# A two-layer convolution block on one core: the places of chains, of a projection and of a rank multiply in a planned order, and the buffers of the last stage

## The chip, the cores and the metric

The kernel runs on one core of one Trainium2 chip. The metric is the device time of one execution in microseconds (us); the median of several runs counts. Lower is better.

## The reference: what is computed

The input x has 4 images of 64 channels, 256 x 256 pixels, float32. Two layers follow each other, each with a residual (x = x + layer(norm(x)), where the norm is a group norm over 32 groups of two channels):

```python
# layer 0, on gn(x)
h = gelu(conv3x3(x, c1_w) + c1_b)
xa, k = split(conv1x1(h, c2_w) + c2_b)            # 64 channels each
xs = gelu(depthwise 1x3 then 3x1 taps of xa)
gate = softmax(mean(xs) @ gate_w.T), the two largest of three kept
out = xs + sum over e of gate_e * w3_e((w2_e k + b2_e) * (w1_e xs + b1_e)) + ...   # ranks 2, 4, 8
return proj(out)
# layer 1, on gn(x)
h = relu(batchnorm(conv3x3(x, quantised w1)))
h = batchnorm(conv3x3(h, quantised w2))
return relu(h + x)
```

The gate of an image needs the mean of xs over the whole image, the norm of layer 1 needs all of an image's layer 0, and the two batch norms need all four images. These are the borders in the program.

## The kernel before: how the work is laid out

**Tiles.** An image is held as 128 partitions (64 channels times two row parities) by 128 row pairs by 256 columns. A step of layer 0 takes four row pairs, so an image has NOCT = 32 steps; a chunk is CPAIR = 8 row pairs (1 MiB), and an image has NCH = 16 chunks.

**The plan.** The functions `plan_front`, `plan_stats`, `plan_out` and `plan_conv1` write no instruction. They put calls into a table under a pair (step, order) with `at`, or the pieces of a generator with `at_each`. The table is then walked sorted by step and order (end of the code shown below), and every call emits its instructions on all engines. The order on TensorE (PE), VectorE (DVE), GpSimd (POOL) and the DMA-issuing SyncE (SP) is kept as written; that of ScalarE (ACT) too, from four steps ahead of conv1. So the order number of a call sets at once the place of its matmuls on PE, of its vector work on DVE and of its DMAs on SP. Image b's layer 0 takes the steps from 32b on; conv1 of layer 1 begins at CONV1 = 128 and takes 65 steps per image. Past CONV1 the last steps of image 3's front are stretched (`tail`).

**Layer 0, the front.** A step of row group n does: two thirds of the 3x3 convolution into PSUM bank c (`front_conv_a`, L452 through `rounds` and `quarter`), the rest of it (`front_conv_b`), a butterfly in PSUM on ACT and DVE (`front_butterfly`, L561 to L563), gelu (`front_h`, L569); three steps later the taps into bank a (`front_taps_a`, `front_taps_b`) and their horizontal part on DVE (`front_taps_h`: L619, L622, L625), gelu into xs (`front_xs`, L639); a step or two later the projection of xs (`front_proj`), whose result is added to x on DVE (L673) and stored to t1_d. Every fourth step `front_k` makes the first rank factor from h (matmuls L649, evacuated on ACT, L657) and `front_q` the second from xs (matmuls L687); DVE multiplies the two (L689) and SP stores them to low_d.

**The tick.** `divide` (L443) emits a one-column memset on POOL that waits for PE's latest matmul, and the next `rounds(..., divided=True)` on PE waits for that memset. `front_conv_b` and `front_taps_b` are such rounds. It parts matmuls into different halves of one bank.

**Layer 0, the back.** As soon as the gate of an image is known (`gate`, a generator of three pieces), `out_slot` takes each half chunk, two row pairs by two: the experts' last matmul on the stored ranks (ps_o, L758), added to t1_d's chunk on DVE (L766), statistics (L768), and a store to y_d. For images 0 to 2 this runs beside the next image's front, one `out_slot` per step from the fourth step on, at order 2. `out_end` makes the norm of layer 1 from the statistics (matmuls ps_m_y, L282, and ps_v_y, L291), `stats_end` that of the next image's layer 0.

**Banks.** Of the PSUM there are four tiles of 4 KB per partition: two of tag c, one of tag a, one of tag p (`BANKS`, L76). `front_proj`, `front_k`, `front_q`, `out_slot` and the small matmuls of gate and norms all use the one p.

**Layer 1.** conv1 reads y_d in chunks through a ring (`dense_in`, four buffers shared with layer 0's `chunk_in`), normalises (ACT), splits and sums pixels (`conv1_add`, `conv1_split`, `conv1_sums`, on ACT, DVE and POOL), and convolves with 128x128 matmuls (L310; banks c, and a or p); `leave` (L335, L336) takes the result out, which goes to h1_d. The second convolution does the same from h1_d. Its results stay in SBUF for the last KEEP = 11 chunks (L58) and go to h2_d for the others (store at L1116).

**The end.** After the second batch norm is known, 64 chunks are finished: y is loaded (L1167), ACT and DVE combine it with h2 (L1179 to L1181), the result is stored (L1183). The chunks that stayed come first; as their buffers come free, the others are reloaded from h2_d (L1188). y is loaded AHEAD = 4 chunks ahead at the emission, into the three or so buffers of the ring and two of a pool `end` in turns of five.

Of the kernel before, what the change touches and what calls it, by code (L numbers as in the profile page):

```python
# [57 lines left out]
KEEP = 11  # L58
# [5 lines left out]
def conv_preact_kernel(ctx: ExitStack, tc: tile.TileContext, io, col128, colset, col64):  # L64
# [7 lines left out]
    ring = ctx.enter_context(tc.tile_pool(name="ring", bufs=4))  # L72
# [27 lines left out]
    def chunk_in(name):  # L100

        t = ring.tile([P, RING], F32, tag="in", name=name)
        return t[:, 0 : CPAIR * PW].rearrange("p (a b) -> p a b", b=PW)

    def dense_in(name, n):

        return ring.tile([P, RING], F32, tag="in", name=name)[:, 0 : n * W].rearrange("p (a b) -> p a b", b=W)
# [30 lines left out]


# [42 lines left out]
    av = const.tile([P, 3, C], F32, name="av")  # L182
    sv_sum, sh_sum, sh_bias, tap_bias = (column(n) for n in ("sv_sum", "sh_sum", "sh_bias", "tap_bias"))
    end, ends = column("end", 2), column("ends", 2)
    outer = const.tile([P, 2, W], F32, name="outer")
    wk = const.tile([P, 2, 2, 32], F32, name="wk")
    both = const.tile([P, P], F32, name="both")
    k_bias = column("k_bias")
    pw3 = const.tile([P, C], F32, name="pw3")
    pb3 = column("pb3", 3)  # L190
    wq = {n: const.tile([P, 5, 2 * P], F32R, name=f"{n}_q") for n in ("w1", "w2")}
# [200 lines left out]
    def stats_group(b, g):  # L392
        if g == 0:
            st_x[b] = stat.tile([P, NG, 6], F32, tag="st_x", name=f"st_x{b}", bufs=1)
        t = x_in[b, g // CG]
        i = g % CG * GP
        nc.vector.bn_stats(st_x[b][:, g, :], t[:, i : i + GP, :])  # L397
# [37 lines left out]
    xs_of, hs, xss, k_sb, pooled, open_c, open_a, open_t = {}, {}, {}, {}, {}, {}, {}, {}  # L435
# [27 lines left out]
    def front_alloc(b, k):  # L463
# [3 lines left out]
        else:  # L467
            xs_of[b, k] = chunk_in(f"x_{b}_{k}")
# [190 lines left out]
    def front_proj(b, n):  # L659

        ps = bank("p", f"ps_p_{b}_{n}")
        proj = c128("proj")

        rounds(
            *(
                [((ps[:, i], i ^ s, i, proj, xss[b, n][:, s].rearrange("p (a b) -> p a b", b=W), (0, GP)), dict(start=True, stop=True))]
                for i in range(2)
                for s in range(2)
            )
        )  # L670
# [24 lines left out]
    def gate(b):  # L695
# [10 lines left out]
        nc.vector.tensor_copy(lg, ps[:, 0:9])  # L706
        mx = stat.tile([P, 1], F32, tag="s2", name=f"mx_{b}")
# [42 lines left out]
    def out_slot(b, k, s):  # L750


        if k == s == 0:
            st_y[b] = stat.tile([P, NG, 6], F32, tag="st_y", name=f"st_y{b}")
# [33 lines left out]
    def conv1_load(b, k):  # L788
        y = y_in[b, k] = dense_in(f"yn_{b}_{k}", CPAIR + 1)
# [68 lines left out]
    def conv1_end(b):  # L858

        h = stat.tile([P, 1, W], F32, tag="h_end", name=f"h_end_{b}")  # L860
# [46 lines left out]
    def plan_front(b):  # L907
# [6 lines left out]
        for n in range(NOCT):  # L914
# [4 lines left out]
            at(g, 5, divide)  # L919
            for step in (g + 1, g + 3):  # L920
                if step >= CONV1:
                    at(place(step), 5, divide)

            at(*((g + 5, 3.2) if b == 0 else (place(g + 4), 6)), front_proj, b, n)
# [13 lines left out]
        for j in range(NOCT // 4):  # L938
            at(place(t + 4 * j + 5), 0.5 if t + 4 * j + 5 < CONV1 else 3.5, front_k, b, j)
            q = place(t + 4 * j + 7) + (2 if e_last and j == NOCT // 4 - 1 else 0)  # L940
            at(q, 3.5 if q == CONV1 - 1 else 10, front_q, b, j)
        e = place(t + NOCT + 3)
        at_each(((e, 2.5), (e, 5.7), (e, 8.7)) if e < CONV1 else ((e + 1, 12.7), (e + 3, 12.7), (e + 5, 12.7)), gate(b))

    def plan_stats(b, t, per):
# [10 lines left out]
        places = (e, 5.4), (e + 1, 5.4), (e + 1, 9.9), (e + 2, 5.4), (e + 2, 9.9), (e + 4, 9.9)  # L956
        at_each(places, stats_end(b))

    def plan_out(b, steps, order, end):

        for k in range(NCH):
# [3 lines left out]
            for i in range(2):  # L965
                at(steps[2 * k + i], order, out_slot, b, k, i)
# [16 lines left out]
    def plan_conv1(b):  # L983
# [4 lines left out]
        for k in range(NCH):  # L988
# [6 lines left out]
            if b == 0 and k < 4:  # L995

                split_at = 11.5 if ready < t + 5 else 13.1
                add, parts, rest = ((t - 3, 9.7), (t - 2, 11.5), (t - 1, 11.5)) if k == 0 else [(ready, split_at)] * 3
                if k:
                    add = affine, 13.06  # L1000
# [12 lines left out]
    for b in range(B):  # L1013
        plan_front(b)
        if b < B - 1:
# [4 lines left out]
            if b == B - 2:  # L1020

                steps[28:] = (CONV1 + 14 + 4 * n for n in range(4))
                end = [(CONV1 + 30 + i, 12.6) for i in range(4)]
            plan_out(b, steps, 2, end)
        else:
            t, e = CONV1 + 36, CONV1 + b * (NG + 1) - 10
            plan_out(b, [t + (e - 6 - t) * n // (NOCT - 1) for n in range(NOCT)], 12.8, [(e - i, 15) for i in (5, 4, 3, 2)])
# [273 lines left out]
```

## Time and profile before

| what | us |
|---|---|
| median of 3 runs | 3307.74 |
| lowest and highest | 3306.99, 3310.03 |
| the profiled execution | 3303.83 |
| its span in the trace | 3302.10 |
| PE busy | 2669.3 (81%) |
| DVE busy | 2675.1 (81%) |
| ACT, POOL busy | 1648.2, 1605.6 |

The profiled execution is the one that the views come from. It took 1.73 us more than the span from its first to its last instruction, and 3.91 us less than the median.

The stages by the trace: layer 0 of image 0 from 66 to 420 us, of image 1 to 773, image 2 to 1127, image 3 to 1480; a passage in which the rest of layer 0 and conv1 share the engines to about 1690; conv1 to 2205; the second convolution from 2225 to 2826; the end from 2841 to 3302. A step of image 0 takes 10.3 us (four of them 41.24), of images 1 to 3 10.9 (43.6).

How to read the views: a line of the timeline gives start, length, engine, the line of the code, the operation, output and inputs, and how many instructions were put together; in brackets stands the idle time before it and what ended it. A line of the waits gives who waited for whom, us in total, times, and the longest. A line of the table by stage gives the stretch, its length, the busy time and number of instructions of PE, PE's weight loads, DVE, ACT and POOL, the granted PE clock (1.00 is full), the share of time that the 16 DMA engines were busy, and GB/s.

### The profile page before, as it was taken

To read this page: it belongs to the slowest core of one execution; us is meant where nothing else is said; L and a number is where in the kernel's file an instruction comes from. 1 tells how busy PE (TensorE), PEld (TensorE's weight loads), DVE (VectorE), ACT (ScalarE), POOL (GpSimd) and SP (SyncE) were. 2 spreads that over 40 slices of the span, in tenths; PEclk is the share of its full clock that TensorE was granted. 3 is DMA by queue.
4 is the path that set the end of the run, shared out by engine and by line. 5 is a ranking of instruction groups with operands and counts; after the bars stand their busy time and mean duration, and the time that the engine had idled before them with its cause. 6 is when DMAs were issued, how large, how long until landed. Compare 5 with 4: busy or idle time off the path is not lost.

```text
span 3302.1 us, 60535 instructions
## 1 busy us (share of the span) xinstructions
PE 2669.3 (81%) x24832; PEld 1750.3 (53%) x24832; DVE 2675.1 (81%) x2810; ACT 1648.2 (50%) x1799; POOL 1605.6 (49%) x1833
## 2 busy tenths in 40 slices
PE   2999999999999999988999998989999999200000
PEld 1555555555555555545667776768787878100000
DVE  7666588878888777768799998979999999866666
ACT  0444444343434444346666666767777777322222
POOL 2544544454445444435678786757777777000000
PEclk9999999999999999999999999999999999655555
DMA  8665689879987767855788896656666664699999
GB/s 304 176 180 128 176 254 282 256 213 280 278 258 213 224 191 219 231 157 189 284 280 303 291 303 210 238 197 229 232 244 232 237 234 155 237 413 413 412 412 386
DMA packets 356453, 838.27 MB, mean 254 GB/s; under 512 B 22288, under 2 KB 284944, under 8 KB 293456
## 3 DMA queue, kind: packets, MB, share of 16 engines
q1 hardware_dynamic: 356176, 834.40, 76.0%
q8 instruction: 195, 3.19, 0.4%
q14 instruction: 82, 0.67, 0.1%
HBM read 493.00 MB, written 341.31 MB: 253 GB/s over the span
## 4 chain that ended last, share of the span: by engine, by line
PE 68%; DMA 12%; DVE 11%; ACT 3%; SPq 3%; issue 2%; POOL 1%; ACTq 0%; POOLq 0%; DVEq 0%
PE ps_h L310 25%; PE ps_c L452 19%; DMA y_end<-y_d 10%; PE ps_a L452 9%; PE ps_h2m L310 3%; PE ps_p L452 3%; PE ps_o L758 3%; PE ps_hm L310 3%; PE ps_k L649 2%; PE ps_q L687 2%; DVE half L356 1%; DVE h L336 1%; DVE st_x L397 1%; SPq L1188 1%; DMA yn<-y_d 1%
## 5 line engine op out<-in xcount | busy, mean ns | idle before, releaser
L310 PE MATMUL ps_h<-half,w_q 128*128 128x512 f32 x4096 | 1032.9, 404 | 21.0 <-DVE h L336 15.3
L310 PEld LDWEIGHTS ps_h<-half,w_q 128*128 128x128 f32 x4096 | 778.4, 191 | 250.8 <-issue 25.3
L375 POOL TENSOR_TENSOR sum<-s,sum 128x640 fp32r<-128x640 f32 (+1 forms) x256 | 558.8, 2203 | 200.2 <-ACT sum L373 194.5
L495 POOL TENSOR_TENSOR v_ring<-x 128x256 f32<-128x256 f32 x1024 | 591.3, 613 | 50.3 <-DMA x<-in_x 46.6
L452 PE MATMUL ps_c<-v_ring,c1s 64*64 64x256 f32 (+1 forms) x6472 | 388.6, 371 | 14.8 <-POOL tick L445 12.6
L452 PE MATMUL ps_c<-v_ring,u 64*64 64x256 f32 (+1 forms) x6472 | 390.1, 370 | 4.8 <-DVE u L423 3.5
L336 DVE SCALAR_TENSOR_TENSOR h<-ps_h,scale_w,m 128x1024 f32<-128x1024 f32 x256 | 327.0, 1277 | 76.5 <-ACT m L335 76.5
L452 PE MATMUL ps_a<-h,av 64*64 64x512 f32 (+1 forms) x3568 | 382.0, 532 | 5.7 <-POOL tick L445 4.4
L569 ACT ACTIVATE h<-ps_c,c1b 128x512 f32<-128x512 f32 x256 | 174.6, 744 | 406.3 <-PE ps_c L452 406.3
L452 PEld LDWEIGHTS ps_c<-v_ring,c1s 64*64 64x64 f32 x6472 | 249.5, 133 | 217.0 <-issue 75.4
L445 POOL MEMSET tick<- 128x1 f32 x132 | 13.0, 98 | 703.5 <-PE ps_a L452 699.0
L452 PEld LDWEIGHTS ps_c<-v_ring,u 64*64 64x64 f32 x6472 | 270.9, 133 | 145.1 <-POOL v_ring L495 67.0
L639 ACT ACTIVATE xs<-t 128x1024 f32<-128x1024 f32 x128 | 135.4, 1058 | 394.2 <-DVE t L625 354.6
L1179 ACT ACTIVATE v<-y_end,shift,gn 128x2048 f32<-128x2048 f32 x64 | 133.8, 2092 | 320.6 <-DMA y_end<-y_d 313.7
L1180 DVE SCALAR_TENSOR_TENSOR h<-h,ss,v 128x2048 f32<-128x2048 f32 x64 | 150.2, 2351 | 159.7 <-ACT v L1179 159.7
L356 DVE TENSOR_TENSOR half<-h,half 128x1280 fp32r<-128x1280 f32 (+1 forms) x128 | 254.5, 2029 | 7.7 <-ACT half L354 7.7
L562 DVE TENSOR_TENSOR ps_c<-m,ps_c 128x512 f32<-128x512 f32 x128 | 89.1, 696 | 204.2 <-ACT m L561 204.2
L452 PEld LDWEIGHTS ps_a<-h,av 64*64 64x64 f32 x3568 | 162.0, 133 | 133.3 <-issue 92.0
L673 DVE TENSOR_TENSOR x<-ps_p,x 128x1024 f32<-128x1024 f32 x128 | 156.2, 1220 | 75.6 <-PE ps_p L452 64.7
L356 DVE TENSOR_TENSOR half<-yn,half 128x1280 fp32r<-128x1280 f32 x80 | 206.1, 2593 | 1.6 <-ACT half L354 1.6
L335 ACT ACTIVATE m<-ps_hm,m,scale_w 128x512 f32<-128x512 f32 x128 | 99.6, 778 | 211.9 <-PE ps_hm L310 190.7
L766 DVE SCALAR_TENSOR_TENSOR y<-ps_o,ob,y 128x1024 f32<-128x1024 f32 x128 | 163.6, 1278 | 17.7 <-PE ps_o L758 14.0
(186 smaller groups left out, 4068.0 us busy)
## 6 DMA issues: line engine op xcount, KB each, us to landing
h_d<-h SPq DMA_DIRECT2D x117, 1024.0 KB, 4.8
h<-h_d SPq DMA_DIRECT2D x64, 1152.0 KB, 7.1
yn<-y_d SPq DMA_DIRECT2D x60, 1152.0 KB, 8.1
xs_in<-in_x SPq DMA_DIRECT2D x64, 1024.0 KB, 9.5
x<-in_x SPq DMA_DIRECT2D x256, 256.0 KB, 5.2
y<-t_d SPq DMA_DIRECT2D x64, 1024.0 KB, 8.5
y_d<-y SPq DMA_DIRECT2D x256, 256.0 KB, 5.2
y_end<-y_d SPq DMA_DIRECT2D x64, 1024.0 KB, 11.1
```

Of the source, the lines that this page charges most:

```text
L310: nc.tensor.matmul(ps[:, 0 : n * HW], w[:, k, m, :], t[:, i + m : i + m + n, c : c + HW], start=(j == 0), stop=(j == len(terms) - 1),)
L336: nc.vector.scalar_tensor_tensor(h.rearrange("p a (b e) -> p e (a b)", e=2), by_two(ps)[:, :, 0 : n * HW], w_scale[w], m.unsqueeze(1).to_b ...
L356: engine.tensor_tensor(lower, y, upper.bitcast(F32), ALU.subtract)
L375: nc.gpsimd.tensor_tensor(tiles[1][:, a:e, :], t, tiles[0][:, a:e, :].bitcast(F32), ALU.subtract)
L452: last[:] = [nc.tensor.matmul(ps[o, at_out[0] : at_out[1], :], w[i], rhs[i], **flags)]
L495: nc.gpsimd.tensor_tensor(v_of(p)[:, o : o + 2, :], *terms[p])
L569: nc.scalar.activation(h.rearrange("p q (c e) -> p e q c", e=2), c[:, t].rearrange("p (e q c) -> p e q c", e=2, q=GP), AF.Gelu, bias=c1_bi ...
L639: nc.scalar.activation(flat(xss[b, n]), flat(open_t.pop((b, n))), AF.Gelu, accum_out=pooled[b][:, n : n + 1])
L673: nc.vector.tensor_tensor(t1, ps, t1, ALU.add)
L766: nc.vector.scalar_tensor_tensor(y, ps.rearrange("p i a b -> p (i a) b"), out_bias[b], y, ALU.add, ALU.add)
L1179: nc.scalar.activation(v, y, AF.Identity, bias=shift[:, b : b + 1], scale=gn2[b][:, 1:2])
L1180: nc.vector.scalar_tensor_tensor(h, h, ss2[:, 0:1], v, ALU.mult, ALU.add)
```

## The change

Five things change together.

- *Results that stay.* KEEP goes from 11 to 14: thirteen buffers of the pool `kept` and one in a new pool `spare`. The ring of four becomes a ring of three plus that `spare`, which serves every fourth use in layer 0 and conv1; in the second convolution the ring has three. To make room, constants and small tiles of layer 0 go to pools that are closed before the second convolution (`lconst`, `lstat`).
- *The end.* The pool for y has six buffers; AHEAD goes from 4 to 8, so nine y loads are emitted by the first turn of the loop in place of five.
- *The projection of image 0* is emitted in two halves by row, the first at order 3.2 and the second at 4.6 around `front_taps_a` (order 4); its `divide` is at 4.4 in place of 5, for steps 5 to 35.
- *The rank factors.* `front_k` goes from order 0.5 of a step to order 11.3 of the step before it; `front_q` from 10 (in one case 3.5) to 11.3, behind `front_taps_h` (11).
- *Chains and sums at the borders.* The gate is cut into four pieces, at other orders; a piece of `stats_end` goes one step on; the first `out_slot` of an image goes from order 2 to 3.4; the pieces of `out_end` for images 2 and 3 stand three and two steps apart in place of one; the first four chunks of conv1 have their add, split and sums at places of their own.

The diff, without the moves of constants between pools:

```diff
@@ -55,7 +55,7 @@
 NLOW = sum(LOWS)
 GN_EPS = 1e-5
 BN_EPS = 1e-5
-KEEP = 11
+KEEP = 14
 QMAX = 127.0
 ROUND = 12582912.0
 
@@ -69,7 +69,8 @@
 
     const = ctx.enter_context(tc.tile_pool(name="const", bufs=1))
     stat = ctx.enter_context(tc.tile_pool(name="stat", bufs=2))
-    ring = ctx.enter_context(tc.tile_pool(name="ring", bufs=4))
+    ring = ctx.enter_context(tc.tile_pool(name="ring", bufs=3))
+    spare = ctx.enter_context(tc.tile_pool(name="spare", bufs=1))
     psum = ctx.enter_context(tc.tile_pool(name="psum", bufs=1, space=PSUM))
     dram = ctx.enter_context(tc.tile_pool(name="dram", bufs=1, space=DRAM))
 
@@ -97,14 +98,17 @@
 
     RING = max(CPAIR * PW, (CPAIR + 1) * W)
 
-    def chunk_in(name):
-
-        t = ring.tile([P, RING], F32, tag="in", name=name)
+    def place_in(name, fourth=False):
+        return (spare if fourth else ring).tile([P, RING], F32, tag="in", name=name)
+
+    def chunk_in(name, fourth):
+
+        t = place_in(name, fourth)
         return t[:, 0 : CPAIR * PW].rearrange("p (a b) -> p a b", b=PW)
 
-    def dense_in(name, n):
-
-        return ring.tile([P, RING], F32, tag="in", name=name)[:, 0 : n * W].rearrange("p (a b) -> p a b", b=W)
+    def dense_in(name, n, fourth=False):
+
+        return place_in(name, fourth)[:, 0 : n * W].rearrange("p (a b) -> p a b", b=W)
 
     layers = ExitStack()
 
@@ -465,7 +471,7 @@
         if c % 5 == 3:
             xs_of[b, k] = chunk_x(f"x_{b}_{k}")
         else:
-            xs_of[b, k] = chunk_in(f"x_{b}_{k}")
+            xs_of[b, k] = chunk_in(f"x_{b}_{k}", c % 5 == 4)
 
     def front_load(b, k):
 
@@ -656,18 +662,29 @@
         k_sb[b, j] = work.tile([P, 2, GF], F32, tag="k", name=f"k_{b}_{j}", bufs=1)
         nc.scalar.activation(flat(k_sb[b, j]), ps.rearrange("p s f -> p (s f)"), AF.Identity, bias=k_bias)
 
-    def front_proj(b, n):
-
-        ps = bank("p", f"ps_p_{b}_{n}")
+    def front_proj(b, n, rows=((0, GP),)):
+
+        if rows[0][0] == 0:
+            open_p[b, n] = bank("p", f"ps_p_{b}_{n}")
+        ps = open_p[b, n]
         proj = c128("proj")
 
-        rounds(
-            *(
-                [((ps[:, i], i ^ s, i, proj, xss[b, n][:, s].rearrange("p (a b) -> p a b", b=W), (0, GP)), dict(start=True, stop=True))]
-                for i in range(2)
-                for s in range(2)
+        for a, e in rows:
+            rounds(
+                *(
+                    [
+                        (
+                            (ps[:, i], i ^ s, i, proj, xss[b, n][:, s].rearrange("p (a b) -> p a b", b=W)[:, a:e], (a, e)),
+                            dict(start=True, stop=True),
+                        )
+                    ]
+                    for i in range(2)
+                    for s in range(2)
+                )
             )
-        )
+        if rows[-1][1] < GP:
+            return
+        del open_p[b, n]
         k, i = n // 2, 4 * (n % 2)
         t1 = xs_of[b, k][:, i : i + 4, 1 : 1 + W].rearrange("p (q s) w -> p s q w", s=2)
         nc.vector.tensor_tensor(t1, ps, t1, ALU.add)
@@ -704,6 +721,7 @@
         nc.tensor.matmul(ps[:, 0:9], spread, c128("gate"), start=True, stop=True)
         lg = stat.tile([P, 9], F32, tag="lg", name=f"lg_{b}")
         nc.vector.tensor_copy(lg, ps[:, 0:9])
+        yield
         mx = stat.tile([P, 1], F32, tag="s2", name=f"mx_{b}")
         nc.vector.tensor_reduce(mx, lg, AX.X, ALU.max)
         nc.vector.tensor_scalar(lg, lg, mx, None, ALU.subtract)
@@ -916,12 +934,17 @@
             at(g, 1, front_conv_a, b, n, (1, 2))
             at(place(g + 1), 3, front_conv_a, b, n, (0, 3))
             at(place(g + 3), 4, front_taps_a, b, n)
-            at(g, 5, divide)
+            at(g, 4.4 if 5 <= g < NOCT + 4 else 5, divide)
             for step in (g + 1, g + 3):
                 if step >= CONV1:
                     at(place(step), 5, divide)
-
-            at(*((g + 5, 3.2) if b == 0 else (place(g + 4), 6)), front_proj, b, n)
+            if b == 0 and n < NOCT - 1:
+
+
+                at(g + 5, 3.2, front_proj, b, n, ((0, 1),))
+                at(g + 5, 4.6, front_proj, b, n, ((1, 2),))
+            else:
+                at(place(g + 4), 6, front_proj, b, n)
             at(g, 7, front_conv_b, b, n, (1, 2))
             at(g, 7.5, front_butterfly, b, n)
             at(place(g + 1), 6.6, front_conv_b, b, n, (0, 3))
@@ -936,11 +959,11 @@
             at(place(g + 3), 11.8, front_xs, b, n)
         e_last = b == B - 1
         for j in range(NOCT // 4):
-            at(place(t + 4 * j + 5), 0.5 if t + 4 * j + 5 < CONV1 else 3.5, front_k, b, j)
+            at(*((t + 4 * j + 4, 11.3) if t + 4 * j + 4 < CONV1 else (place(t + 4 * j + 5), 3.5)), front_k, b, j)
             q = place(t + 4 * j + 7) + (2 if e_last and j == NOCT // 4 - 1 else 0)
-            at(q, 3.5 if q == CONV1 - 1 else 10, front_q, b, j)
+            at(q, 11.3, front_q, b, j)
         e = place(t + NOCT + 3)
-        at_each(((e, 2.5), (e, 5.7), (e, 8.7)) if e < CONV1 else ((e + 1, 12.7), (e + 3, 12.7), (e + 5, 12.7)), gate(b))
+        at_each(((e, 2.5), (e, 7.2), (e, 7.6), (e, 11.4)) if e < CONV1 else ((e + n, 12.7) for n in (1, 3, 4, 6)), gate(b))
 
     def plan_stats(b, t, per):
 
@@ -953,7 +976,7 @@
 
             at(step, 5.8 if b > 1 and (step - NOCT * (b - 1)) in (3, 5, 6) else 3.5, stats_group, b, g)
         e = t + int(NG / per) + 1
-        places = (e, 5.4), (e + 1, 5.4), (e + 1, 9.9), (e + 2, 5.4), (e + 2, 9.9), (e + 4, 9.9)
+        places = (e, 5.4), (e + 1, 5.4), (e + 1, 9.9), (e + 2, 5.4), (e + 3, 5.4), (e + 4, 9.9)
         at_each(places, stats_end(b))
 
     def plan_out(b, steps, order, end):
@@ -963,7 +986,8 @@
                 ahead = steps[2 * k - 3] if k > 1 else steps[0] - 2
                 at(max(ahead, steps[2 * k] - 4) if b == B - 2 else ahead, order + 0.2, call, b, k)
             for i in range(2):
-                at(steps[2 * k + i], order, out_slot, b, k, i)
+
+                at(steps[2 * k + i], 3.4 if order == 2 and k == i == 0 else order, out_slot, b, k, i)
         at_each(end, out_end(b))
 
     conv1_pool, halves, sums = [], [], []
@@ -994,10 +1018,12 @@
             at(affine, 5.6 if affine < t else 13.05 if b == 0 and k < 4 else 12.2, conv1_affine, b, k)
             if b == 0 and k < 4:
 
-                split_at = 11.5 if ready < t + 5 else 13.1
-                add, parts, rest = ((t - 3, 9.7), (t - 2, 11.5), (t - 1, 11.5)) if k == 0 else [(ready, split_at)] * 3
-                if k:
-                    add = affine, 13.06
+                add, parts, rest = (
+                    ((t - 3, 9.7), (t - 2, 11.5), (t, 5.5)),
+                    ((t + 2, 5.5), (t + 2, 11.5), (t + 2, 13.2)),
+                    ((t + 4, 5.5), (t + 4, 11.5), (t + 4, 13.2)),
+                    ((affine, 13.06), (ready, 13.1), (ready, 13.2)),
+                )[k]
                 at(*add, conv1_add_early, b, k)
                 at(*parts, conv1_split, b, k)
                 at(*rest, conv1_sums, b, k)
@@ -1020,11 +1046,11 @@
             if b == B - 2:
 
                 steps[28:] = (CONV1 + 14 + 4 * n for n in range(4))
-                end = [(CONV1 + 30 + i, 12.6) for i in range(4)]
+                end = [(CONV1 + 30 + 3 * i, 12.6) for i in range(4)]
             plan_out(b, steps, 2, end)
         else:
             t, e = CONV1 + 36, CONV1 + b * (NG + 1) - 10
-            plan_out(b, [t + (e - 6 - t) * n // (NOCT - 1) for n in range(NOCT)], 12.8, [(e - i, 15) for i in (5, 4, 3, 2)])
+            plan_out(b, [t + (e - 6 - t) * n // (NOCT - 1) for n in range(NOCT)], 12.8, [(e - i, 15) for i in (5, 3, 1, -1)])
         plan_conv1(b)
 
     kept_to = {mybir.EngineType.PE, mybir.EngineType.SP, mybir.EngineType.DVE, mybir.EngineType.Pool}
@@ -1088,10 +1114,14 @@
     halves2 = split_tiles(halves_pool, "2")
     sums2 = [sum_tiles(halves_pool, f"2{i}", 6) for i in range(2)]
     s2 = halves_pool.tile([P, CPAIR + 1, HW], F32, name="s2")
-    h2, st_h2 = {}, {}
+    h2, st_h2, h2_place = {}, {}, count()
 
     def chunk_h2(b, k):
-        h2[b, k] = kept.tile([P, CPAIR, W], F32, tag="h2", name=f"h2_{b}_{k}", bufs=KEEP)
+        n = next(h2_place) % KEEP
+        if n == KEEP - 1:
+            h2[b, k] = dense_in(f"h2_{b}_{k}", CPAIR, True)
+        else:
+            h2[b, k] = kept.tile([P, CPAIR, W], F32, tag="h2", name=f"h2_{b}_{k}", bufs=KEEP - 1)
         return h2[b, k]
 
     def conv2(d):
@@ -1156,14 +1186,15 @@
 
     halves_stack.close()
     end = ctx.enter_context(tc.tile_pool(name="end", bufs=2, reuse_waits="tile"))
-    AHEAD = 4
+    MORE = 6
+    AHEAD = 3 + MORE - 1
 
     def end_load(i):
         b, k = steps[i]
-        if i % 5 < 3:
+        if i % (3 + MORE) < 3:
             y_of[i] = dense_in(f"y_end_{b}_{k}", CPAIR)
         else:
-            y_of[i] = end.tile([P, CPAIR, W], F32, tag="y", name=f"y_end_{b}_{k}")
+            y_of[i] = end.tile([P, CPAIR, W], F32, tag="y", name=f"y_end_{b}_{k}", bufs=MORE)
         nc.sync.dma_start(y_of[i], y_d[b][:, k * CPAIR : (k + 1) * CPAIR, :])
 
     for i in range(AHEAD):
```

## The prediction

> **What bounds the kernel now.** I read the page's row of forty slices first (which engine is full when), then busy time by stage, then waits and timeline of the stages that the change touches, and last the chain of work at the end.
>
> ```profile
> PE   2999999999999999988999998989999999200000
> ...
> PEclk9999999999999999999999999999999999655555
> ```
>
> TensorE is full until slice 34; then come six slices without a matmul. By stage (window, then PE, PEld, DVE, ACT and POOL busy, granted clock, DMA share, GB/s):
>
> ```profile
> 420.00:773.00 353.00, 346.60 (x4832) 188.56 (x4828) 296.34 (x384) 142.60 (x202) 157.46 (x308) 1.00 0.84 251
> 1480.00:1690.00 210.00, 189.21 (x824) 132.98 (x821) 173.47 (x183) 127.67 (x128) 133.99 (x82) 0.94 0.70 240
> 2225.00:2826.00 601.00, 598.33 (x2545) 477.81 (x2543) 572.54 (x510) 452.02 (x440) 435.78 (x259) 1.00 0.60 220
> 2876.00:3250.00 374.00, 0.00 (x0) 0.00 (x0) 227.52 (x98) 102.75 (x50) 0.00 (x0) 0.50 1.04 412
> 793.36:796.77 3.41, 3.41 (x28) 1.55 (x28) 3.31 (x5) 0.74 (x1) 0.00 (x0) 0.50 1.00 297
> ```
>
> Image 1 of layer 0 (first row) and the second convolution (third) keep PE at 98 to 99.6%: any PE wait there is paid in full. The passage into conv1 (second row) leaves PE 21 of 210 us idle. The end (fourth row) is the transfers': 412 GB/s, DVE at 61%. The last row is one window just behind a PE wait of 1.87 us: it runs at half clock.
>
> The place that decides is a step whose `front_q` fills bank p in images 1 to 3 (start, length, engine, line):
>
> ```profile
> 562.59 1.92 PE L687 MATMUL ps_q<-xs,m 128*32 128x512 f32 x16
> 563.61 0.69 DVE L563 TENSOR_TENSOR ps_c<-m,ps_c 128x512 f32<-128x512 f32 x1
> 564.44 1.96 PE L452 MATMUL ps_c<-v_ring,u 64*64 64x256 f32 x32
> 564.61 1.28 DVE L689 SCALAR_TENSOR_TENSOR k<-ps_q,m,k 128x1024 f32<-128x1024 f32 x1 [0.30 <-PE ps_q L687]
> 565.80 1.27 DVE L619 SCALAR_TENSOR_TENSOR t<-ps_a,m,t 128x1020 f32<-128x1020 f32 x1
> ...
> 566.33 1.13 PE L758 MATMUL ps_o<-ranks,wm 32*128 32x512 f32 x4
> ...
> 567.11 1.28 DVE L622 SCALAR_TENSOR_TENSOR t<-ps_a,m,t 128x1020 f32<-128x1020 f32 x1
> ...
> 568.43 0.17 DVE L625 TENSOR_TENSOR t<-t,ends 128x8 f32<-128x8 f32 x1
> 568.61 1.28 DVE L766 SCALAR_TENSOR_TENSOR y<-ps_o,ob,y 128x1024 f32<-128x1024 f32 x1
> ```
>
> Bank p is one buffer. The k multiply (L689) empties it at 565.89; ps_o, the next user, starts at 566.33, when PE reaches it. PE does not wait: the cover is 32 matmuls.
>
> [...] 13 half-clock windows of 3.41 us (or pairs) stand between 420 and 2050 us, all behind PE waits; but already 1.87 us of idleness in a window did it once and once not, 2.09 us did, and waits of 1.5 to 1.8 us mostly did not. [...] the trace shows no matmul overtaking a waiting one. [...] The trace of the end shows 412 GB/s, reads and writes together[...].
>
> **The change part by part.** The reckoning is against the profiled run: span 3302.10 us plus 1.73 around it, 3303.83; the median shown is 3.9 higher, and I add that last. Minus is a gain.
>
> *1. front_q from order 10 to 11.3.* PE's order stays; on DVE the k multiply now stands behind L619, L622 and L625 of the same step. In a step without q, L619 starts 0.60 us after L563 (575.54, 576.14), so the multiply ends 0.60 + 1.31 (L619 to L622) + 1.32 (L622 to L625) + 0.18 + 1.28 = 4.69 us after L563, and ps_o starts some 0.05 later: 4.74. Before it starts at 2.65 to 2.72 (566.33 − 563.61). PE waits 2.05 us, and behind ps_o in PE's order stand the next step's convolution, taps and projection: nothing fills it. It strikes where the step after q has an `out_slot`: seven times each in images 1 and 2, six in image 3. 20 x 2.05 = **+41.0**. The earlier L625 frees `xs` sooner, but PE there waits for xs in no more than 0.4 us an image. Upper bound of the wait 2.3 (ps_o's own semaphore delays), lower 1.8 (some matmuls late anyway): 36 to 46.
>
> *Clock.* A wait of 2.05 falls wholly into one window with chance (3.41 − 2.05)/3.41 = 0.40; a window at half clock costs half of 3.41, 1.7 us of PE work. 20 x 0.40 x 1.7 = **+13.6** (none: 0; all: 34).
>
> *2. Image 0: projection in halves, division at 4.4.* The tick on POOL waits for PE's last taps matmul, and 31 times PE then stands (wait line of window 66 to 420: total, times, longest):
>
> ```profile
> PE ps_c L452 <- POOL tick L445: 11.0, 33, 0.6
> ```
>
> Now the second half (four matmuls, 0.5 us) stands between. 31 x 0.33 = −10.2. Against it: in the seven steps behind q the first half, four matmuls earlier than all eight were, waits for the later k multiply, 0.49 us each, +3.4; and the projection's add, t_d's store and POOL's pads behind that come later, +1.8 by my estimate. **−5** (−14.6, all of the 0.47 that a step of image 0 loses to PE, to +2). In images 1 to 3 the projection stays whole; there ticks at 4.4 cost nothing, since POOL has finished before ps_c asks (PE waits 1.6 us for it in images 1 and 2 together).
>
> *3. Image borders.* The gate chain is cut in four, the first `out_slot` of an image goes from 2 to 3.4. Before, that slot waited 1.27 to 1.87 us. Now ps_g stands behind the second convolution half and its DVE chain (2.6 us) behind taps and k multiply: I expect 3 us and a half window, less the waits of 1.71 and 1.34 that go. **+2** in three borders (−4 to +6). `stats_end`'s fifth step moves one step on, with nobody near it: 0.
>
> *4. Into conv1, and its chains.* PE's waits between 1430 and 1690 us, by start, length and releaser: 1430.8 2.92 (k), 1458.2 4.05 (y), 1471.2 1.70, 1500.7 4.14 (tick), 1513.3 2.83, 1542.1 2.73 (h), 1589.7 4.70 (mv_y), 1609.3 2.09, 1655.9 1.50; later 2010.1 3.31 and 2015.8 2.81 (image 3's chain). With ten half windows behind them, 33 + 17 = 50 us stand there at most. The k evacuation moves ahead of ACT's next work, −2.9; q at step 127 to 11.3 takes 1.9 of 4.05 and the 1.70 behind it, −3; sums and adds now behind the ticks instead of ahead of them, −3.5; the gate's fourth piece −2; the chain of image 2 over steps three apart instead of one, −6.5 with its windows; that of image 3 two apart, −6.5. Sum **−25** (−12 to −50, since what DVE leaves undone there it does a step later).
>
> *5. The end.* Three more chunks stay (14), so three stores in conv2 and three reloads fall away, and nine y loads instead of six come before the stretch that transfers bound. The stores lay beside PE (DMA 0.60 busy in conv2): 0. At the end a pair of chunks takes 15.25 us:
>
> ```profile
> 2875.11 14.39 DMA y_end<-y_d
> ...
> 2890.35 14.42 DMA y_end<-y_d
> ```
>
> A chunk is 7.63 us for 3 MiB (y, h2, out), 2.54 a MiB. Three reloads less are 7.6; three y loads earlier another 7.6, if conv2's queues take them in time (buffers free from about 2796 to 2826, first output at 2845). Eleven chunks at the tail already go without reload, so not all of it is seen: **−13** (−10 to −15.2). The ring's loss of one buffer in conv2 meets a prefetch of three chunks ahead, as many as there are: 0; if a load then waits for the affine of its slot, up to +5.
>
> Sum: 41.0 + 13.6 − 5 + 2 − 25 − 13 = +13.6. 3303.83 + 13.6 + 3.9 = **3321 us**, own range 3312 to 3332.
>
> **Rivals.** *A, faster: the waits into conv1 go whole.* Where: 1430 to 1690 and 2010 us, part 4. If each shift takes its wait and the half window behind it, 50 instead of 25 go, the sum is −11.4, and the time 3296. For it: 17 of the 50 are windows, which go with any wait that falls below about 1.8 us. Against: the waits have different releasers, and DVE holds 83% there. It decides from 38.6 us gained there (the sign) and 45 us (faster by over 0.2%). *B, no change: the clock never falls* behind the new ps_o waits. Sum 0, 3307.7. For it: waits up to 1.8 us mostly kept the clock, and 2.05 is close; against: 2.09 dropped it. *C, slower still: every such wait costs a window*, 20 x 1.7 = 34, sum +34: 3342. Against: only waits inside one window showed it. *D: the end is limited by the last stores and gains nothing*: sum +26.6, 3334. Against: the chain there is y loads almost wholly. That the moved multiply isn't waited for (the change not doing what step 1 says) would need ps_o to use another bank; it has one.
>
> **How the numbers follow.** Forecast 0.40, A 0.27, B 0.20, C 0.08, D 0.05. 0.2% is 6.6 us, about what a measurement of this kernel can tell from no change. Faster is A: 0.27; same is B: 0.20; slower the rest: 0.53. The range goes from A's far part (3288, with 8 us more from parts 2 and 5) to D and parts 2 and 3 at their dear ends (3337).
>
> **What would show it.** In the profile after: PE ps_o waiting for DVE k (the moved multiply) about 20 times, 2 us each, in images 1 to 3, and half-clock windows behind a part of them; ps_c's wait for the tick in image 0 gone; total PE waits between 1430 and 1690 down by about half; the first output 3 chunks nearer the end at an unchanged period of 15.25 a pair. I am wrong if ps_o does not wait (then some 55 us too high), or if the waits into conv1 fall by more than 39 us.

## The result and the profile after

The changed kernel takes 3339.29 us (median of 4 runs, 3332.81 to 3342.94), the kernel before 3307.36: a ratio of 1.0094, with a 95% interval of 1.0073 to 1.0114. It is slower, as forecast, but by 32 us in place of 14, and the time lies 2 us above the range that was given.

The profiled execution has a span of 3341.0 us against 3302.1. Both are at the edge of their runs (3342.82 in all, 3.5 over the median; 3303.83, 3.5 under), so that some 7 of the 39 us between the traces are chance. Marked by the same events in both traces (the butterflies of DVE, the last matmuls, the first ACT of the end), the difference splits so:

| stretch | before, us | after, us | difference | of it PE waits | of it half clock |
|---|---|---|---|---|---|
| start to the first butterfly | 71.91 | 73.32 | +1.4 | | |
| image 0 | 323.14 | 323.16 | 0.0 | −2.8 | 0 |
| images 1 to 3, to the last butterfly | 1076.32 | 1135.64 | +59.3 | +32.0 | +29.0 |
| passage and conv1 | 734.22 | 727.64 | −6.6 | −6.6 | −3.4 |
| second convolution, with the norm before it | 619.99 | 619.87 | −0.1 | 0 | 0 |
| end, with the norm before it | 476.47 | 461.38 | −15.1 | | |

("Half clock" is half the length of the half-clock windows. What the last two columns leave over is PE at work.)

The step that the prediction showed now looks so (the timeline of the changed kernel, the same columns):

```profile
481.01 1.27 DVE L625 SCALAR_TENSOR_TENSOR t<-ps_a,m,t 128x1020 f32<-128x1020 f32 x1
...
482.31 1.28 DVE L628 SCALAR_TENSOR_TENSOR t<-ps_a,m,t 128x1020 f32<-128x1020 f32 x1
483.63 0.17 DVE L631 TENSOR_TENSOR t<-t,ends 128x8 f32<-128x8 f32 x1
483.71 1.28 DVE L706 SCALAR_TENSOR_TENSOR k<-ps_q,m,k 128x1024 f32<-128x1024 f32 x1
...
485.05 1.79 PE L776 MATMUL ps_o<-ranks,wm 32*128 32x512 f32 x4 [1.94 <-DVE k L706]
486.77 2.93 PE L458 MATMUL ps_c<-v_ring,c1s 64*64 64x256 f32 x32
```

The k multiply stands behind both taps, and ps_o starts 0.06 us after its end. Behind the wait the 32 matmuls of ps_c take 2.93 us; before they took 1.96: the clock has fallen. The waits of PE over images 1 to 3, and the table by stage (length, PE, PEld, DVE, ACT, POOL, granted clock, DMA share, GB/s):

```profile
PE ps_o L776 <- DVE k L706: 38.0, 20, 2.0
```

```profile
420.00:773.00 353.00, 333.22 (x4490) 178.09 (x4485) 278.52 (x362) 133.24 (x189) 146.40 (x285) 0.97 0.80 236
485.40:488.80 3.40, 3.40 (x24) 1.29 (x24) 1.89 (x2) 0.00 (x0) 0.00 (x0) 0.50 0.91 331
```

Twenty waits, 1.9 us each (2.05 were forecast); in a stretch of 353 us, 420 to 773 us in both traces, PE gets through 4490 matmuls where it did 4832. Between the first butterfly of image 1 and the last of image 3 the clock is halved in 21 windows of 3.41 us, before in 4. Of the 20 waits, 14 are followed by half clock, one of them for two windows: 15 windows, 25.6 us. The other six windows, 10.2 us, stand behind the first `out_slot` of images 0 to 2 at its new place ("issue": the profile shows nothing that PE waits for there):

```profile
PE ps_o L776 <- issue: 9.2, 3, 3.1
```

These three waits are 3.05 to 3.07 us long; in the kernel before that slot waited 1.27 to 1.87 us, and one window stood behind the three.

In image 0 the tick's wait is down from 11.0 us to this:

```profile
PE ps_a L458 <- DVE t L628: 3.0, 13, 0.6
PE ps_c L458 <- POOL tick L451: 2.6, 9, 0.5
```

and yet image 0 is as long as before. A step of both kernels shows a part of the reason; first the kernel before, then the changed one:

```profile
199.78 1.28 DVE L622 SCALAR_TENSOR_TENSOR t<-ps_a,m,t 128x1020 f32<-128x1020 f32 x1
200.40 1.04 PE L452 MATMUL ps_p<-xs,m 64*64 64x512 f32 x8
...
201.26 1.90 PE L452 MATMUL ps_a<-h,av 64*64 64x512 f32 x20
...
203.49 1.09 PE L452 MATMUL ps_c<-v_ring,c1s 64*64 64x256 f32 x16 [0.33 <-POOL tick L445]
```

```profile
200.81 1.28 DVE L628 SCALAR_TENSOR_TENSOR t<-ps_a,m,t 128x1020 f32<-128x1020 f32 x1
201.43 0.61 PE L458 MATMUL ps_p<-xs,m 64*64 64x256 f32 x8
...
202.24 1.95 PE L458 MATMUL ps_a<-h,av 64*64 64x512 f32 x20 [0.20 <-DVE t L628]
...
203.99 0.64 PE L458 MATMUL ps_p<-xs,m 64*64 64x256 f32 x8
204.37 0.10 POOL L451 MEMSET tick<- 128x1 f32 x1 [4.74 <-PE ps_a L458]
204.52 1.09 PE L458 MATMUL ps_c<-v_ring,c1s 64*64 64x256 f32 x16
```

From ps_p to ps_c both take 3.09 us. Half a projection should have brought the taps (ps_a) forward by 0.4 us. But bank a, one buffer too, is read by DVE's second tap until 202.09; the taps start 0.81 us after ps_p in place of 0.86, the tick that waits for them is as late as ever, and ps_c still starts 0.15 us after the tick. The new wait has taken the place of the old one.

Not all steps are like this one. Measured from tick to tick, of every four steps one is 0.43 us shorter than before (3.0 us in all) and two are as long. In one of these two, the step behind `front_q`, the halves alone do gain 0.21 us, and the later k multiply takes it back. The fourth step is up to 0.56 us longer (1.7 in all), since the tick stands behind a pad of POOL (L488) that comes later. One more step is 1.6 us longer: there the matmul ps_m_x of the next image's norm waits 1.4 us for the projection's add, which now comes behind the second half.

The end, by stage (the full stretch, and its last 21 us):

```profile
2930.00:3290.00 360.00, 0.00 (x0) 0.00 (x0) 233.36 (x101) 104.56 (x50) 0.00 (x0) 0.50 1.04 412
3320.00:3341.00 21.00, 0.00 (x0) 0.00 (x0) 0.75 (x1) 0.00 (x0) 0.00 (x0) 0.50 0.93 302
```

The rate is the same 412 GB/s. Counted from the first ACT of the end, the ACT work of the 21st chunk starts 30 us sooner than before (at 100.0 in place of 130.1), since y is loaded four chunks further ahead; but the store of that chunk lands no sooner (163.7 and 163.3). The gain of 15 us comes from bytes: from the first ACT on, 170.3 MiB are moved in place of 175.1, which at the 2.54 us per MiB of the prediction is 12 us by estimate. The tail itself has become longer: when the last y has landed, stores of nine chunks are still under way or to come, before of five, and stores alone run at 302 GB/s.

### The profile page after: what moved, and what is told of

Read it like the earlier page. It is cut to its first block, busy times and chain, and to the rows that moved or that the text cites. A ratio compares the mean times of both kernels' runs of the same rounds, so it can differ in the third digit from the quotient of the medians.

```text
span 3341.0 us, 60996 instructions
## 1 busy us (share of the span) xinstructions
PE 2700.4 (81%) x25080; PEld 1770.9 (53%) x25080; DVE 2672.9 (80%) x2810; ACT 1648.4 (49%) x1799; POOL 1606.2 (48%) x1833
## 4 chain that ended last, share of the span: by engine, by line
PE 59%; DVE 18%; SPq 8%; DMA 6%; ACT 4%; issue 3%; POOL 1%; POOLq 0%; DVEq 0%; ACTq 0%
PE ps_h L316 23%; PE ps_c L458 15%; PE ps_a L458 8%; SPq L1219 4%; PE ps_h2m L316 3%; PE ps_o L776 3%; PE ps_p L458 3%; PE ps_hm L316 2%; DVE t L628 2%; ACT h L575 2%; DVE t L625 2%; DVE half L362 2%; SPq L1214 2%; PE ps_k L655 2%; DVE h L342 2%
## 5 line engine op out<-in xcount | busy, mean ns | idle before, releaser
L458 PE MATMUL ps_c<-v_ring,c1s 64*64 64x256 f32 (+1 forms) x6472 | 404.4, 383 | 5.4 <-POOL tick L451 5.0
L458 PE MATMUL ps_a<-h,av 64*64 64x512 f32 (+1 forms) x3568 | 390.9, 542 | 6.4 <-DVE t L628 4.0
L458 PEld LDWEIGHTS ps_c<-v_ring,c1s 64*64 64x64 f32 x6472 | 256.8, 137 | 211.8 <-issue 84.5
```

The source lines that it names most:

```text
L458: last[:] = [nc.tensor.matmul(ps[o, at_out[0] : at_out[1], :], w[i], rhs[i], **flags)]
```

## The experiments

The theory after the result: the moved multiply costs two things of the same order, its waits and the clock behind them; the projection's halves run into bank a; in the passage to conv1 most waits turn up at another matmul and few go away. The rivals are given with each run. Medians; the kernel before of the same chip stands beside them.

**front_q back.**

```diff
-            at(q, 11.3, front_q, b, j)
+            at(q, 3.5 if q == CONV1 - 1 else 10, front_q, b, j)
```

> The changed kernel with one part undone: front_q stands again at order 10 (3.5 at the last step of the front), so that DVE takes the k multiply ahead of the taps. Theory (the moved multiply costs its 20 waits of 1.9 us and the half-clock windows behind them, some 60 us in images 1 to 3): 3276 to 3290, no PE wait of ps_o on the k multiply, and 4 to 7 half windows between the starts of image 1 and of the passage instead of 21. Rival (the new gate pieces and the first out_slot at 3.4 carry a large share): the time falls only to 3305 to 3320, and long waits at the image borders remain.

Measured: 3283.21 against 3306.69 (0.9923, 0.9908 to 0.9937), 56 us below the changed kernel. After the setup PE waits for the k multiply once, 0.8 us, and 6 windows of half clock stand in images 1 to 3. One line made the change slower; all the rest of it together is worth 24 us. Of the rival one half is there: the first `out_slot` of three images still waits 3.6 us each time, and five of the six windows stand behind these waits. No run puts that slot back alone.

**front_q alone**, and the same with its wait filled by work.

```diff
-            at(q, 3.5 if q == CONV1 - 1 else 10, front_q, b, j)
+            at(q, 11.3, front_q, b, j)
```

> The kernel before with one part of the change alone: front_q at order 11.3 everywhere. Theory (38 us of waits and about 29 us of clock): 3360 to 3378, ps_o waiting on the k multiply 20 times or a few more, 1.9 us each, and some 15 to 20 more half windows. Rival (the clock is lost to the other moves, and these waits cost their length alone): 3340 to 3348.

```diff
-        rounds(*conv_tile(... 0, 0, ...), *conv_tile(... 1, 1, ...))
+        again = first and b > 0 and n % 4 == 0 and (n >= 8 or n == 0 and b > 1)
+        for _ in range(2 if again else 1):
+            rounds(*conv_tile(... 0, 0, ...), *conv_tile(... 1, 1, ...))
```

> The same as the kernel with front_q alone moved, and in the 20 steps behind a front_q in which an out_slot follows, the first group of convolution matmuls (32 matmuls, about 1.8 us of PE) is issued twice; the second pass starts the sums anew. PE so works through most of the wait. Theory (idleness in the wait is what halves the clock): the waits shrink to some 0.2 us, the half windows go back to those of the kernel before, and the time is 3338 to 3350, 25 to 30 below front_q alone. Rival 1 (the clock doesn't hang on these waits): the same as front_q alone, 3360 to 3378. Rival 2 (the wait isn't for the multiply as such but follows PE, so the work comes on top): 3390 to 3415.

Measured: 3376.12 (1.0203, 1.0188 to 1.0218) and 3358.25 (1.0152, 1.0131 to 1.0173). The waits and the stage of images 1 to 3 of front_q alone:

```profile
PE ps_o L758 <- DVE k L689: 50.4, 21, 6.1
```

```profile
397.00:1545.00 1148.00, 1078.18 (x14576) 581.73 (x14564) 865.19 (x1104) 439.64 (x619) 470.87 (x916) 0.97 0.76 222
```

and of the filled one:

```profile
PE ps_o L760 <- DVE k L691: 17.7, 13, 6.1
```

```profile
397.00:1522.00 1125.00, 1087.29 (x15220) 596.05 (x15208) 865.47 (x1104) 440.05 (x620) 471.01 (x916) 0.99 0.77 227
```

Both came out dearer than expected (front_q alone at the top of its range, the filled one 8 us over its own): at the old places of the gate the multiply also meets an image's first out_slot, a wait of up to 6.1 us. The comparison between the two is what tells: in the traces PE's waits fall by 32 us and its work grows by 32, so that this part costs the same; the half clock costs 37.6 us in one and 13.7 in the other, and the spans of the stage differ by those 23. With front_q alone, 16 of the 18 waits of 1.9 us are followed by half clock. In the filled kernel no step with added work is; its eight windows all stand at the borders of the images. The same time, spent working and not waiting, keeps the clock. Rival 1 (no clock in it) and rival 2 (work on top) are both out; by the medians the gap is 17.9 us (the runs of one kernel take 3374 to 3378 us, of the other 3354 to 3365).

**The halves alone**, and with a tap of image 0 left out.

```diff
-            at(g, 5, divide)
+            at(g, 4.4 if 5 <= g < NOCT + 4 else 5, divide)
...
+                at(g + 5, 3.2, front_proj, b, n, ((0, 1),))
+                at(g + 5, 4.6, front_proj, b, n, ((1, 2),))
```

> The kernel before with one part alone: the projection of image 0 in halves and its tick at order 4.4. Theory (PE reaches the taps' first matmuls 0.4 us earlier, but their bank a is only then given back by DVE's second tap, so the taps and the tick start when they did): 3304 to 3310, a step of image 0 as long as before (10.3 us), PE ps_a waiting on DVE's second tap about 0.2 us in most steps of image 0. Rival (the halves hide the ticks and gain 10 us, which in the changed kernel the later k multiply gave back): 3294 to 3300.

Measured: 3303.01 against 3306.69 (0.9990, 0.9983 to 0.9997), image 0 322.0 us against 323.1. That lies between the two ranges, 1 us under the theory's and 3 over the rival's; the trace has ps_a waiting on the second tap (3.1 us, 13 times) as the theory has it. One trace can't tell 1.1 us from chance here: among the five kernels that share one program for image 0 (front_q back and the four repairs below) it takes from 321.9 to 323.2 us. The ratio rests on 20 runs and more; by its interval this kernel is 1 to 6 us faster. Then the base with the tap left out, and the halves on top:

```diff
+        if b > 0:
             nc.vector.scalar_tensor_tensor(
                 t[:, :, 0 : W - 1], ps[:, :, 1:W], sh[:, 2:3], t[:, :, 0 : W - 1], ALU.mult, ALU.add
             )
```

> The kernel before, with the second of the two shifted taps on DVE left out in image 0 (the right neighbour of the 1x3 filter; a part of the computation is missing there). Alone it should change nothing, since PE bounds image 0 and waits for the tick, not for bank a: image 0 (first to 33rd butterfly) 320 to 323.5 us, as in the kernel before (323.1). It is the base for the next kernel.

> The same with the projection of image 0 in halves and the tick at order 4.4; the same tap is left out in image 0. Theory (with the tap in place, bank a comes free too late for the taps' matmuls to start earlier, and that alone ate the gain of the halves): DVE now gives bank a back 1.3 us earlier, the taps start 0.4 us earlier, and image 0 takes 309 to 315 us, 8 to 13 less than the kernel with the tap left out and the projection whole. Rival (the two halves cost PE as much as the tick did, in matmul overhead): 321 to 324, no difference between the two.

Measured: 3304.51 and 3298.47 against 3306.39 (0.9993, 0.9984 to 1.0002; 0.9977, 0.9968 to 0.9986); image 0 takes 323.1 and 318.2 us. With the tap in place the halves take 1.1 us off image 0, without it 4.9. A step of the last one, and a line of an earlier step:

```profile
170.65 0.34 POOL L482 TENSOR_SCALAR x<-zeros,gn 128x16 f32<-128x16 f32 x1 [4.54 <-DMA t_d<-x]
...
197.21 1.27 DVE L619 SCALAR_TENSOR_TENSOR t<-ps_a,m,t 128x1020 f32<-128x1020 f32 x1
...
199.14 0.61 PE L452 MATMUL ps_p<-xs,m 64*64 64x256 f32 x8
199.57 1.90 PE L452 MATMUL ps_a<-h,av 64*64 64x512 f32 x20
...
201.79 1.09 PE L452 MATMUL ps_c<-v_ring,c1s 64*64 64x256 f32 x16
```

The taps start 0.43 us behind ps_p and the step from ps_p to ps_c is 2.65 us in place of 3.09, the 0.44 that was looked for: in such steps bank a was the obstacle. Of every four steps three are now shorter by 0.36 to 0.44 us. The sum over image 0 misses its range (8 to 13) all the same. The fourth step is longer, by up to 1.0 us: the tick stands in POOL's queue behind the pad of the first line, which waits for the store of t1 behind the later add. And the step with the next norm's matmul is longer by 1.4. So the theory holds in three steps of four, and the later add, the second obstacle, takes back a part.

**The end alone** (KEEP, the pools, MORE and AHEAD as in the diff of the change).

> The kernel before with one part alone: 14 results stay, the ring of three with a spare, six buffers for y and loads eight chunks ahead. Theory: the end takes 451 us in place of 466 and nothing else moves, 3289 to 3294. Rival (the ring of three or the moved pools cost something in layer 0 or conv1 that the sum of the change hides): 3295 to 3305.

Measured: 3290.52 against 3306.39 (0.9952, 0.9937 to 0.9967); the end takes 452.3 us in the trace. The ring of three costs nothing in layer 0 or conv1: they take as long as before, but for a half-clock window more in image 1 and two in the passage, against waits that are 3 us shorter there.

**The borders alone** (gate, norms, first out_slot, front_k, conv1's first sums as in the diff of the change, front_q as before).

> The kernel before with one part alone: the gates, norms, first out_slots, the k factor's place and the first sums of conv1 at the new places; front_q stays where it was. From the changed kernel with front_q back, which has the same plan there: from the first butterfly of image 3's last step to the end of conv1 about 9 us less, the image borders about 4 more. Theory (the waits are moved more than removed): 3297 to 3305. Rival (the 25 us of the forecast are there, but front_q's move ate them): 3280 to 3290.

Measured: 3293.77 (0.9962, 0.9948 to 0.9976), 12.6 us, between the two ranges: half of what the forecast took. The passage and conv1 take 725.1 us in place of 734.2; images 1 to 3 take 1077.8 in place of 1076.3, so that the 4 us expected at the borders are not there. These waits stand in the passage:

```profile
PE ps_h L310 <- DVE h L336: 14.3, 6, 6.1
PE ps_o L759 <- DVE var_y L293: 4.7, 1, 4.7
PE ps_q L687 <- DVE y L767: 4.1, 1, 4.1
```

The gate of image 3 had made ps_h wait 2.73 us before; behind its moved last piece it is 6.1. The norm of image 2 had made its mean wait 4.7 us; now its variance does, since ps_v was put right ahead of an out_slot in the one bank p. The last line is front_q in the front's last step, which this kernel leaves at 3.5.

**Repairs**, on the changed kernel with front_q at order 10: the last step left at 11.3; then image 3's gate at its old steps; or image 2's norm with two pieces a step earlier; then both.

```diff
-            at(q, 11.3, front_q, b, j)
+            at(q, 11.3 if q == CONV1 - 1 else 10, front_q, b, j)
```

> The changed kernel with front_q back at order 10 in all steps but the last of the front, where it stays at 11.3 (against the experiment with all of them back, in which it stands at 3.5 there and PE waits 4.1 and 1.7 us with half windows behind). Theory (there, nothing of the back shares the bank right behind, so 11.3 is the better place): 3274 to 3281, 3 to 8 us below all back. Rival (the wait comes back as one of ps_o on the k multiply, 1.9 us and a window): 3281 to 3286, no gain.

```diff
-        ... ((e + n, 12.7) for n in (1, 3, 4, 6)) ...
+        ... ((e + n, 12.7 + m) for n, m in ((1, 0), (3, 0), (3, 0.01), (5, 0))) ...
```

> The same with the gate of image 3 at its old steps: its last piece, a chain of small DVE instructions, at the fifth step of the passage, as in the kernel before, not at the sixth. There PE waited 2.73 us for DVE in the kernel before and 4.9 to 6.1 behind the moved piece. Theory (the piece's new place is the dearer one): 2 to 5 us below the kernel with front_q at 11.3 only in the last step, and the wait of ps_h under 3 us. Rival (the chain costs PE the same wherever it stands, since DVE is short of time there): within 2 us of it.

```diff
-                end = [(CONV1 + 30 + 3 * i, 12.6) for i in range(4)]
+                end = [(CONV1 + 30 + n, 12.6) for n in (0, 3, 5, 8)]
```

> The kernel with front_q at 11.3 only in the last step, and the norm of image 2 with its third and fourth piece one step earlier (0, 3, 5 and 8 steps in place of 0, 3, 6 and 9), so that its ps_v matmul does not stand right ahead of an out_slot in the one bank p. Theory (spreading that chain put a wait of 4.7 us of ps_o on the norm's variance where one of 4.7 us on its mean had been): that wait goes with the half clock behind it, 4 to 8 us less. Rival (DVE hands back late there whatever stands ahead): a wait of 3 us or more moves to another matmul near, within 2 us.

> The last two edits together, as the best version that the experiments point to. If both theories hold, 6 to 13 us below the kernel with front_q at 11.3 only in the last step: 3264 to 3273. If both rivals hold, 3274 to 3281.

Measured against 3306.13: 3278.17 (0.9915, 0.9900 to 0.9930), 3274.55 (0.9903, 0.9889 to 0.9918), 3276.36 (0.9900, 0.9883 to 0.9917) and 3272.68 (0.9896, 0.9881 to 0.9911). The first is 5 us below front_q all back by the medians, within what its theory said. But the two were measured against different runs of the kernel before; by the ratios the gap is 2.6 us and the intervals overlap, so that this gain is not shown. In the trace the waits of 4.1 and 1.7 us have become one of 2.5. With the norm moved, the 4.7 us on the variance are gone, but 2.7 stand on the next matmul of the same chain:

```profile
PE ps_v_y L297 <- DVE d_y L294: 4.1, 2, 2.7
```

That is mostly the rival. With the gate moved, the median falls as the theory said, but the wait behind the chain is 4.5 us, not under 3; only with both moved is it 2.7. The intervals of these four overlap, so the single repairs are not shown; the last has the lowest median, 1.0% under the kernel before, and is faster than both. A part of its lead may be chance: in its trace images 1 to 3, which are the same program in all four, are 4 to 5 us shorter than in the other three.

## Why the prediction was wrong

Its direction and its main mechanism, the twenty waits, were right. The term that failed first is the clock behind these waits, at about half of its size; three smaller terms were wrong in the same direction. In the traces, in us:

| term | forecast | measured |
|---|---|---|
| waits of ps_o on the k multiply | +41.0 | +38.0 |
| half clock behind these waits | +13.6 | +25.6 |
| image 0 | −5 | 0.0 |
| image borders, with their windows | +2 | +8.7 |
| the step of `stats_end` | 0 | −3.0 |
| into conv1, from image 3's last steps on | −25 | −14.5 |
| the end | −13 | −15.1 |
| the start | not named | +1.4 |
| the rest | | −2.1 |
| sum | +13.6 | +39.0 |

By the medians the sum is +32.

- *Waits of ps_o*: twenty of them, 1.9 us each, in the steps that were named.
- *The clock*: the step that failed is "a wait of 2.05 falls wholly into one window with chance ... 0.40", an estimate from the lengths of wait and window, which puts at nothing every wait that is split between two windows. The half-clock windows of the trace lie on a fixed grid of 3.4133 us, so that each wait can be placed in it. Ten of the twenty lay wholly in one window (eight were forecast), and all ten were followed by half clock. But of the ten split ones four were too, with 1.40 to 1.64 us in the later window; and one of the fourteen cost two windows. With front_q alone it was 11 of 11 whole and 5 of 7 split waits of this length. Where the waits fall in the grid may be partly chance, and the 10 us between the four runs may come from there (their mean clock goes from 0.914 in the longest to 0.917 in the shortest); with one of the four traced, this is not shown.
- *Image 0*: the step counted what PE waits for last (the tick) and did not ask what the work moved ahead of it would wait for. In the trace of before, DVE's second tap ends at 201.06 and ps_a starts at 201.26, so 0.2 us of room were there for a move of 0.43; in the changed kernel ps_a starts 0.15 us after the tap's end, which leaves 0.05. The later add was in the forecast at 1.8; it costs about 3.3 (1.7 in the steps with the pad and 1.6 in the one with the norm). The later k multiply costs 2.4 with front_q alone (image 0 takes 325.5 us), where 3.4 were taken.
- *Image borders*: the wait of 3 us came as forecast, three times, but with two windows each in place of half a window; and the waits of the gate that were to go came back next to it (1.5 and 0.7 us in image 1, 1.9 in image 2).
- *stats_end*: its fifth piece, put at nothing, had made ps_q wait 1.5 us in two images, and these waits are gone in the kernels with the piece at its new place, whether front_q is moved or not.
- *Into conv1*: image 3's last steps bring 7.9 (the k evacuation and front_q, with two windows), the rest of the passage 6.6. The norm of image 3 brings nearly what was forecast. That of image 2 brings nothing of its 6.5: it kept its 4.7 us on another matmul. The gate's last piece makes ps_h wait 4.9 us in place of 2.7, where a gain of 2 was taken. The bound was drawn ("what DVE leaves undone there it does a step later"); the value taken was too near the good side.
- *The end*: right in mechanism and size, −15.9 alone by the medians.
- *The start*: the other kernels with the new pools show −0.2 to +2.1 there, those without −0.4 to +1.2, so that it can be chance.

Of the rivals, C (every wait costs a window) was the nearest, at 3342. Its clock term, 34, is nearer to 25.6 than 13.6 is, but that its time comes so close is luck: it is 8 us too high there, and has the same errors in the other terms.

What is not settled: what the first `out_slot` would cost at its old place with all the rest of the change, and how much each move in the passage to conv1 is worth alone; the runs there differ by less than their intervals.

## What to carry to other kernels

Where an order is written by hand and a buffer is single, the place of the instruction that empties it sets a deadline: ask which user of the buffer comes next, on which engine, and what stands ahead of the emptying one. On TensorE a wait of 1.9 us cost nearly twice its length where the clock fell behind it (14 of 20 here, with 1.7 us for half of a window of 3.41); the same time filled with work kept the clock (in all 20 steps with added work). And before counting a removed wait as gained, look at the second thing that the same instruction waits for: its slack is the most that can come out.

## What the runs showed of the hardware

- *The half-clock windows are on a fixed grid, and some half of a window idle was mostly enough.* In all fourteen traces of this case the starts of the half-clock windows lie on a grid of 3.4133 us, to within 0.005. Of the windows of this grid between 100 us and the last matmul, take those that ran at full clock themselves, and sort them by how long PE was idle in them (the matmul ends in the traces are modelled, so these times are not exact). With 0.6 to 1.3 us idle none of 235 was followed by half clock, with 1.3 to 1.8 us 29 of 127, with 1.8 to 2.1 us 46 of 57, above that all 137. In the traces of before and after alone the counts are 0 of 37, 6 of 24, 13 of 14 and all 23. So in these runs 1.8 us or more of idleness in a window of 3.41 was mostly followed by half clock, and 0.6 to 1.3 us never.
- *Small DVE instructions stretched beside POOL.* The last piece of the gate takes 2.74 us for images 0 to 2, when POOL does nothing, and 8.68 us for image 3, beside POOL's large two-input operations (timeline of the changed kernel):

```profile
1597.56 2.42 POOL L362 TENSOR_TENSOR half<-yn,half 128x1024 fp32r<-128x1024 f32 x1 [2.33 <-ACT half L360]
...
1598.10 1.92 DVE L734 TENSOR_SCALAR gate<-gate,tot 128x9 f32<-128x9 f32 x1
```

A multiply of nine columns, 0.23 us for the other images, here ends when POOL's operation does (1600.02 and 1599.98). What stretches it is not shown: no run tried it apart. At its old step the same piece is stretched too: 7.5 us in the kernel before, 8.1 in the repair with the gate at its old steps. So its length alone does not explain why PE waits 2.7 us behind it in one and 4.5 in the other.
